# A graph-attention kernel on one core: 18 steps of layer 1 kept for the last change of layers, a spare PSUM bank, another order of the last closings, values by two node tiles

## The chip, the core and the metric

The kernel runs on one core of one Trainium2 chip. The core has five engines with instruction streams of their own: PE (TensorE, matmuls, with its weight loads shown apart as PEld), DVE (VectorE), ACT (ScalarE), POOL (GpSimd) and SP (SyncE, which here only issues DMAs). [...] The metric is the device time of one execution in microseconds (us); before the change it was 3778.08 us, the median of three runs (3776.47 to 3779.17).

## What is computed

Eight batches of 2048 nodes with 256 features go through two graph layers over one adjacency matrix. Cut to what matters:

```python
# layer 0: attention in 4 heads of 64, softmax inside each chunk of 256 keys, summed over 8 chunks
scores = clip(q @ k.T / 8, -10, 10); scores = where(adj == 0, -10, scores)
attn   = softmax(scores, over the 256 keys of a chunk)
y      = layernorm(sum over chunks of attn @ v, @ Wo + x)
x1     = layernorm(x + y)
# layer 1: graph attention, 4 heads of 64
Wh = x1 @ W;  e = leaky_relu(s_src[i] + s_dst[j], 0.2), -inf where adj == 0
h  = elu(softmax(e over j) @ Wh)
out = layernorm(x1 + h)
```

All is fp32. Each fp32 matmul of the program appears as two PE instructions in the profile.

## The kernel before

**Slots.** Layer 0 of a batch is cut into 64 slots (`SLOTS`): 4 query chunks `q` of 512 nodes, times 2 head pairs, times 8 key chunks. `i` is a slot's place in its query chunk, 0 to 15. Slot `s` issues the scores of slot `s + 1` (L385, tile `ps`), their clip and mask on DVE (L396, `pr`), `product(s, 0)` and `product(s, 1)` (L422, one for each head of the pair, tile `pc`), and between these the exponentials of slot `s + 1` on ACT (L408). ACT copies each `pc` out of PSUM (`raw`, L429); in the next slot DVE takes reciprocals of the sums (L437) and POOL multiplies and adds (L444, L446).

**Layer 1 rides along.** Layer 1 of batch `b - 1` (object `lower`, class `Layer1`) runs beside layer 0 of batch `b`. It has 8 units (2 halves of the nodes times 4 heads) of 16 tiles. A tile needs one DVE instruction (`make`, L741: `e` from `srow`, `gd` and the edge mask `et`) and 32 PE instructions (`use`, L763, tile `pa`). `step` makes two tiles and uses two; `make` stays two tiles ahead. At the end of a unit, ACT copies `pa` to `sums` (L775) and a generator `close` is put on `lower.tail`: its five pieces (`dn` L788 and L789, two lots of four scalings L795, exponential and relu L800 and L801, and `h` L803 on DVE) are taken one at a time by `rest(1)`, the first thing that each `step` does.

**Change of layers.** After slot 63 a written list `order` interleaves the last query chunk's output, norms and values, `factors` (three pieces: the last, `rows`, stores the rows of layer 1 to DRAM and has POOL scale `waug`, L686 and L688) and, for batches 0 to 6, the projections of the next batch. For the last batch (7) there is no next batch: slots 50 to 63 run without layer 1 steps (`LATE = 14`), and these 14 steps of batch 6's layer 1 stand in `order` instead; the last of them and `rest(5)`, which finishes the tail, come after `rows`. Then a new `Layer1` is built. Its constructor issues, on SP and in this order, three edge loads (L723) and one row load `srow` (L712). An edge buffer (4 of them) comes free when the two tiles that read it are made.

**Layer 1 alone.** The layer 1 of batch 7 then runs by itself, 64 steps, with the closings of batch 6 (`CLOSING_ALONE`) and of batch 7's first half (`ENDING`) between its steps. A closing of a group of 512 nodes loads `x1g`, adds it to `h` (L828), takes statistics (L487, L490, L495 to L498) and applies them (L502), then stores. Groups 2 and 3 of batch 7 need the last unit and are closed after step 63.

**Values.** The class `Between` holds what follows a query chunk's attention. Its `values(us)` multiplies `x1T` by layer 1's weights (L581, tile `pw`) and has ACT copy the result to `waug` (L588) and `sd` (L592). For one node tile, `pw` lies in bank `psM`; for two, in one of the two-bank tiles.

**PSUM.** `two_banks` turns between `psA0` and `psA1` (two banks each: `ps`, `pp`, `pv`, `po` of four tiles, `pw` of two tiles). `psC` is one bank for `pc`. `one_bank` turns between `psL0` and `psL1`, which hold `pa` whenever layer 1 runs. `psM` is one bank for `po` of two tiles, `pw` of one tile, and the small products of the change of layers. In batch 0, where no layer 1 runs, `product(s, 1)` takes `one_bank`; in all other slots both products take `psC` in turn.

Of the kernel before, what the change touches and what calls it, by code (L numbers as in the profile page):

```python
# [8 lines left out]
F32 = mybir.dt.float32  # L9
# [4 lines left out]
AF = mybir.ActivationFunctionType  # L14
ALU = mybir.AluOpType
AX = mybir.AxisListType

P = 128
CH = 512
# [3 lines left out]
def adj_resnorm_kernel(  # L23
# [19 lines left out]
    nc = tc.nc  # L43
    B, N, F = x.shape
    H, D = a_src.shape
    NT = N // P
# [3 lines left out]
    D1 = D + 1  # L50
# [5 lines left out]
    QT = CH // P  # L56
# [8 lines left out]
    SLOTS = NCH * QS  # L65
    UNITS = [(m, h) for m in range(len(BANKS)) for h in range(H)]
    FIRST = [sum(BANKS[:m]) for m in range(len(BANKS))]
    TILES = len(UNITS) * NT
    STEP = TILES // SLOTS
    LATE = 14  # L70
    WIDE = max(BANKS)
    JG = 2
    AHEAD_E = 3
# [31 lines left out]
    def two_banks(shape, name):  # L105

        turn_of[0] ^= 1
        return psA.tile(shape, F32, tag=f"psA{turn_of[0]}", name=name)

    def one_bank(shape, name, kind=F32):  # L110

        bank_of[0] ^= 1
        return psL.tile(shape, kind, tag=f"psL{bank_of[0]}", name=name)


    qT = big.tile([P, KC, N], F32, tag="qT", name="qT")
# [85 lines left out]
    def send():  # L202
        while outgoing:
            outgoing.pop(0)()
# [202 lines left out]
        pr = probs[s][u]  # L407
        nc.scalar.activation(pr, pr, AF.Exp, scale=0.125)  # L408

    def product(s, k, alone):  # L410
        q, hp, c = where[s]
        if k == 0:
            raws[s] = small.tile([P, 2, QT, D1], F32, tag="raw", name="raw")

        if alone and k:
            pc = one_bank([P, QT, D1], "pc")
        else:
            pc = psC.tile([P, QT, D1], F32, tag="psC", name="pc")
        for i in range(QT):
            for u in range(KT):  # L420
                for z in range(2):
                    nc.tensor.matmul(  # L422
                        pc[z * D : (z + 1) * D, i, :],
                        lhsT=probs[s][u][:, k, i * P + z * D : i * P + (z + 1) * D],
                        rhs=vaug[:, KT * c + u, 2 * hp + k, :],
                        start=(u == 0),
                        stop=(u == KT - 1),
                    )
        nc.scalar.copy(raws[s][:, k], pc)  # L429
# [81 lines left out]
    class Between:  # L511
# [60 lines left out]

        def values(self, us):
            n, t = len(us), QT * self.g + us[0]
            if n == 1:
                pw = psM.tile([P, 1, CH], F32, tag="psM", name="pw")
            else:
                pw = two_banks([P, 2, CH], "pw")
            for k, u in enumerate(us):
                for c in range(KC):  # L580
                    nc.tensor.matmul(  # L581
                        pw[:, k, : F + 2 * H],
                        lhsT=self.x1T[:, c, u * P : (u + 1) * P],
                        rhs=w1_sb[:, c, :],
                        start=(c == 0),
                        stop=(c == KC - 1),
                    )
            nc.scalar.copy(  # L588
                self.waug[:, t : t + n, :, :D],
                pw[:, :, :F].rearrange("p k (h d) -> p k h d", h=H),  # L590
            )
            nc.scalar.copy(  # L592
                self.sd[:, :, t : t + n], pw[:, :, F : F + 2 * H].rearrange("p k x -> p x k")
            )
# [16 lines left out]
        4: lambda o: o.output((2, 3)),  # L611
        7: lambda o: o.a.apply(o.y),
        11: lambda o: o.finish(),
        14: lambda o: o.values((0,)),
        15: lambda o: o.values((1,)),
    }

    WIDE_BESIDE = {
# [16 lines left out]
    }  # L635
    LATER_AHEAD = {0: lambda o: o.load()}
    LATER_BESIDE = {2: lambda o: o.turn()}
    LATER_BEHIND = {i: lambda o, i=i: o.values((i - 5,)) for i in range(5, 9)}

    BESIDE_0 = {i: steps for i, steps in BESIDE.items() if i != 14} | {15: BESIDE[14]}  # L640
    BEHIND_0 = {i: step for i, step in BEHIND.items() if i != 14} | {15: BEHIND[14]}

    def factors(b, sd, waug):

# [52 lines left out]
    class Layer1:  # L697
# [54 lines left out]
        def use(self):  # L752
            k = self.used
            n, j = k // NT, k % NT
            m, h = UNITS[n]
            if j == 0:
                self.pa = [
                    psL.tile([P, QT, D1], F32, tag=f"psL{i}", name="pa") for i in range(n_banks)
                ]
            e = self.e.pop(k)  # L760
            for i in range(BANKS[m]):
                for z in range(2):
                    nc.tensor.matmul(  # L763
                        self.pa[i // QT][z * D : (z + 1) * D, i % QT, :],
                        lhsT=e[:, i * P + z * D : i * P + (z + 1) * D],
                        rhs=self.waug[:, j, h, :],
                        start=(j == 0 and i % QT == 0),
                        stop=(j == NT - 1 and i % QT == QT - 1),
                        skip_group_check=True,
                    )  # L770
            self.used += 1
            if j == NT - 1:
                raw = small.tile([P, WIDE, D1], F32, tag="sums", name="sums", bufs=1)
                for i, pa in enumerate(self.pa):
                    nc.scalar.copy(raw[:, i * QT : (i + 1) * QT, :], pa)  # L775
                self.tail.append(self.close(n, raw))
# [41 lines left out]
    class Close:  # L818
# [12 lines left out]
        def finish(self):  # L831
            o = blocks.tile([P, QT, F], F32, tag="y", name="o")
            self.n.apply(o)
            outgoing.append(lambda: nc.sync.dma_start(out=by_node(out, self.b, self.g), in_=o))

    class Closing:


# [3 lines left out]
        def do(self, s, beside=True, behind=True):  # L842
            for g, step in self.table.get(s, ()):
                if step == "load" and behind:
                    self.of[g] = Close(self.b, g)
                elif step == "finish" and behind:
                    self.of[g].finish()
                elif step == "add" and beside:
                    self.of[g].add()
                elif step == "stats" and beside:  # L850
                    self.of[g].n.stats((0, 1, 2, 3))


    masks = Masks()
# [6 lines left out]
    for g in range(NCH):  # L861
        _, _, keys, values, queries = groups[g]
# [48 lines left out]
        39: [(1, "add")],  # L911
        40: [(0, "finish"), (1, "stats")],
        42: [(1, "finish")],
        SLOTS - 1: [(2, "load"), (3, "load")],
        SLOTS: [(2, "add"), (2, "stats"), (3, "add"), (3, "stats"), (2, "finish"), (3, "finish")],
    }
    lower = None
    for b in range(B):
# [15 lines left out]
        for s in range(SLOTS):  # L934
# [5 lines left out]
            if i == 0:  # L940
                before = group
                group = Between(b, q - 1, sd, waug) if q else None
                wide = 0 < q < NCH - 1
                ahead = {} if wide else AHEAD
                if wide:
                    beside, behind = WIDE_BESIDE, WIDE_BEHIND
                else:
                    beside, behind = (BESIDE, BEHIND) if b else (BESIDE_0, BEHIND_0)
                later_beside, after = (LATER_BESIDE, LATER_BEHIND) if q > 1 else ({}, {})
            if before and later_beside and i in LATER_AHEAD:  # L950
                LATER_AHEAD[i](before)
# [24 lines left out]
                    step(group)  # L976
            elif closing:
                closing.do(s, behind=False)
            product(s, 0, not lower)
            if s + 1 < SLOTS:  # L980
                for u in range(KT):
                    exps(s + 1, u)
# [2 lines left out]
                    lower.step()  # L985
            elif masks.left():
                masks.step()
            product(s, 1, not lower)

            if before and i in after:  # L990
                after[i](before)
# [35 lines left out]
        if b + 1 < B:  # L1027
            (k0, v0, q0), (l1, t1, k1, v1, q1), (l2, t2, k2, v2, q2), (l3, t3, k3, v3, q3) = turns
            rest = [lambda: lower.rest(1)] if lower else []
            first = [] if b else [lambda: before.values((1,))]  # L1030
            order = [begin, *rest, l1, *rest, *first, lambda: before.values((2, 3))]
            order += [*rest, ctx, *rest, *rest, k0]
            order += [steps[0], t1, steps[1], v0, steps[2], steps[3], l2, k1, steps[4], q0]
            order += [steps[5], v1, t2, l3, steps[6], q1, steps[7], k2, steps[8], steps[9], t3, v2]
            order += [lambda: [load_slab(s) for s in range(3)], fs[0], q2, fs[1], k3, fs[2], v3]
            order += [lambda: scores(0), q3, lambda: [exps(0, u) for u in range(KT)]]
        else:

            step = lower.step
            order = [begin, lambda: before.values((2, 3)), steps[0], step, ctx, step, steps[1], step]  # L1040
            order += [steps[2], step, steps[3], step, steps[4], step, steps[5], step, steps[6], step]
            order += [steps[7], step, steps[8], step, steps[9], step, fs[0], step, fs[1], step, fs[2]]
            order += [step, lambda: lower.rest(5)]
            assert sum(p is step for p in order) == LATE
        for piece in order:
            send()
            piece()
        send()
        lower = Layer1(b, gd, waug)

    closing, ending = Closing(B - 2, CLOSING_ALONE), Closing(B - 1, ENDING)
    closing.do(-1)
    for _ in range(STEP):
        lower.make()
    for s in range(SLOTS + 1):
        send()
        if s < SLOTS:
            lower.step()
        else:
            lower.rest(5)  # L1060
        closing.do(s)
        ending.do(s)
    send()


# [40 lines left out]
```

## Time and profile before

| what | value |
|---|---|
| median of three runs | 3778.08 us |
| the profiled execution | 3776.29 us |
| its span, first to last instruction | 3774.5 us |
| granted TensorE clock, mean | 0.993 |
| slots of batch 7, with what lies before them in that batch | 3134.1 to 3516 us |
| change of layers after batch 7 | 3516 to 3577.8 us |
| layer 1 of batch 7 alone | 3577.8 to 3755.6 us |
| last closings, to the end of the span | 3755.6 to 3774.5 us |

The profile is of one execution; times in it count from the span's start. A row of the timeline gives start, length, engine, line, operation, the tile written and the tiles read, how many instructions were merged, and in brackets the engine's idle time just before, with what ended it. Matmuls overlap one another, so the mean length of one says nothing of their rate; the distance between the starts of two groups does. In the chain of waits, overlaps are cut out, so its lengths add up.

### The profile page before, as it was taken

To read this page: it belongs to the slowest core of one execution; us is meant where nothing else is said; L and a number is where in the kernel's file an instruction comes from. 1 tells how busy PE (TensorE), PEld (TensorE's weight loads), DVE (VectorE), ACT (ScalarE), POOL (GpSimd) and SP (SyncE) were. 2 spreads that over 40 slices of the span, in tenths; PEclk is the share of its full clock that TensorE was granted. 3 is DMA by queue.
4 is the path that set the end of the run, shared out by engine and by line. 5 is a ranking of instruction groups with operands and counts; after the bars stand their busy time and mean duration, and the time that the engine had idled before them with its cause. 6 is when DMAs were issued, how large, how long until landed. Compare 5 with 4: busy or idle time off the path is not lost.

```text
span 3774.5 us, 159666 instructions
## 1 busy us (share of the span) xinstructions
PE 3664.0 (97%) x72100; PEld 2741.3 (73%) x72100; DVE 3133.7 (83%) x4202; ACT 1988.0 (53%) x3665; POOL 1365.5 (36%) x1202
## 2 busy tenths in 40 slices
PE   9999999999999999999999999999999999999786
PEld 5656677776777777776777767777677777776676
DVE  5877489986999689895998959988699977988798
ACT  4666455555555555555555545555455555555322
POOL 1445234333433343333443324433334333334300
PEclk9999999999999999999999999999999999999998
DMA  6652333333333343333433334333433333433354
GB/s 163 152 117 69 78 98 109 105 75 112 106 108 105 86 119 102 104 93 88 133 97 98 100 89 135 109 100 78 113 107 107 105 80 112 115 97 84 95 154 128
DMA packets 672060, 398.46 MB, mean 106 GB/s; under 512 B 427280, under 2 KB 591504, under 8 KB 671376
## 3 DMA queue, kind: packets, MB, share of 16 engines
q1 hardware_dynamic: 621376, 354.54, 35.6%
q10 hardware_dynamic: 50000, 33.70, 2.8%
q8 instruction: 564, 9.24, 1.0%
q14 instruction: 120, 0.98, 0.1%
HBM read 331.22 MB, written 56.89 MB: 103 GB/s over the span
## 4 chain that ended last, share of the span: by engine, by line
PE 86%; DVE 5%; issue 3%; ACT 3%; DMA 1%; POOL 1%; SPq 0%; ACTq 0%; DVEq 0%; POOLq 0%
PE pc L422 26%; PE ps L385 24%; PE pa L763 22%; PE pp L329 5%; PE po L537 3%; PE pw L581 3%; PE pv L345 2%; DVE e L741 2%; ACT y L502 1%; DVE pr L396 1%; ACT pr L408 1%; DMA xp<-in_x_dram 0%; PE pm L246 0%; ACT qT L337 0%; SPq L279 0%
## 5 line engine op out<-in xcount | busy, mean ns | idle before, releaser
L396 DVE SCALAR_TENSOR_TENSOR pr<-ps,slab 128x1024 f32<-128x1024 f32 x1024 | 1194.3, 1207 | 211.1 <-PE ps L385 207.7
L422 PEld LDWEIGHTS pc<-vaug,pr 128*64 128x64 f32 x32768 | 1039.5, 138 | 406.4 <-issue 313.6
L741 DVE SCALAR_TENSOR_TENSOR e<-srow,gd,et 128x1024 f32<-128x1024 f32 x1024 | 1273.1, 1286 | 10.4 <-PE pa L763 5.8
L422 PE MATMUL pc<-vaug,pr 128*64 128x65 f32 x32768 | 1155.9, 224 | 14.3 <-ACT raw L429 7.7
L763 PE MATMUL pa<-waug,e 128*64 128x65 f32 x32768 | 1069.8, 224 | 41.0 <-DVE e L741 36.4
L763 PEld LDWEIGHTS pa<-waug,e 128*64 128x64 f32 x32768 | 1015.1, 139 | 60.1 <-DVE e L741 45.5
L408 ACT ACTIVATE pr<-pr 128x1024 f32<-128x1024 f32 x1024 | 1038.2, 1055 | 32.8 <-DVE pr L396 26.4
L385 PE MATMUL ps<-qT,kT 64*128 64x512 f32 x4096 | 1023.2, 616 | 3.5 <-DVE pr L396 2.9
L429 ACT COPY raw<-pc 128x260 f32<-128x260 f32 x1024 | 380.5, 372 | 1222.7 <-PE pc L422 1178.7
L444 POOL TENSOR_TENSOR part<-raw,rd 128x512 f32<-128x512 f32 x448 | 467.9, 1044 | 1407.5 <-DVE rd L437 1389.4
L446 POOL TENSOR_TENSOR acc<-acc,part 128x512 f32<-128x512 f32 x448 | 575.0, 1283 | 35.2
L385 PEld LDWEIGHTS ps<-qT,kT 64*128 64x128 f32 x4096 | 349.9, 186 | 326.6 <-issue 229.6
L437 DVE RECIPROCAL rd<-raw 128x8 f32<-128x8 f32 x512 | 100.8, 197 | 132.1 <-ACT raw L429 129.6
L444 POOL TENSOR_TENSOR acc<-raw,rd 128x512 f32<-128x512 f32 x64 | 66.7, 1043 | 339.3 <-DVE rd L437 339.3
L581 PE MATMUL pw<-w_sb,x1T 128*128 128x264 f32 x512 | 139.8, 409 | 6.1 <-DVE x1T L291 5.0
L795 ACT ACTIVATE sums<-sums,dn 128x64 f32<-128x64 f32 x512 | 134.0, 337 | 9.7 <-DVE dn L789 9.3
L497 POOL TENSOR_TENSOR rs_c<-rs_c,nhalf 128x4 f32<-128x4 f32 x32 | 54.0, 1687 | 223.8 <-DVE off_c L496 223.8
L537 PE MATMUL po<-wo_sb,qT 128*128 128x256 f32 x512 | 125.5, 390 | 3.1 <-DVE qT L464 2.8
L329 PE MATMUL pp<-xT,wk_sb 128*128 128x512 f32 x256 | 119.3, 609 | 7.9 <-ACT qT L337 6.6
L329 PE MATMUL pp<-xT,wq_sb 128*128 128x512 f32 x256 | 116.2, 597 | 0.0
L345 PE MATMUL pv<-wv_sb,xT 128*128 128x256 f32 x512 | 115.9, 379 | 0.0
L581 PEld LDWEIGHTS pw<-w_sb,x1T 128*128 128x128 f32 x512 | 92.4, 193 | 27.5 <-DVE x1T L291 5.3
(94 smaller groups left out, 1853.1 us busy)
## 6 DMA issues: line engine op xcount, KB each, us to landing
et<-edgeD SPq DMA_DIRECT2D x512, 256.0 KB, 3.1
slab<-clipD SPq DMA_DIRECT2D x512, 128.0 KB, 3.1
srow<-rowD SPq DMA_DIRECT2D x64, 512.0 KB, 5.0
xg<-in_x_dram SPq DMA_DIRECT2D x32, 512.0 KB, 5.3
x1D<-y ACTq DMA_DIRECT2D x32, 512.0 KB, 4.4
x1g<-x1D SPq DMA_DIRECT2D x32, 512.0 KB, 5.2
out_dram<-o SPq DMA_DIRECT2D x32, 512.0 KB, 3.3
ctxD<-acc ACTq DMA_DIRECT2D x56, 256.0 KB, 2.5
```

The costliest lines, as they stand in the source:

```text
L329: nc.tensor.matmul(pps[c], lhsT=w[:, kc, c * P : (c + 1) * P], rhs=st["xT"][:, kc, :], start=(kc == 0), stop=(kc == KC - 1),)
L385: nc.tensor.matmul(ps[:, k, :], lhsT=kT[rows, hp, t * P : (t + 1) * P], rhs=qT[rows, hp, cols], start=True, stop=True,)
L396: nc.vector.scalar_tensor_tensor(pr, pss[u], -CLIP, slab[:, u, :].unsqueeze(1).to_broadcast([P, 2, CH]), op0=ALU.max, op1=ALU.min,)
L408: nc.scalar.activation(pr, pr, AF.Exp, scale=0.125)
L422: nc.tensor.matmul(pc[z * D : (z + 1) * D, i, :], lhsT=probs[s][u][:, k, i * P + z * D : i * P + (z + 1) * D], rhs=vaug[:, KT * c + u, 2 * ...
L429: nc.scalar.copy(raws[s][:, k], pc)
L444: nc.gpsimd.tensor_mul(part, raw[:, :, :, :D], rd.to_broadcast([P, 2, QT, D]))
L446: nc.gpsimd.tensor_add(accv, accv, part)
L537: nc.tensor.matmul(po[:, k, :], lhsT=qT[:, c, t * P : (t + 1) * P], rhs=wo_sb[:, c, :], start=(c == 0), stop=(c == KC - 1),)
L581: nc.tensor.matmul(pw[:, k, : F + 2 * H], lhsT=self.x1T[:, c, u * P : (u + 1) * P], rhs=w1_sb[:, c, :], start=(c == 0), stop=(c == KC - 1),)
L741: nc.vector.scalar_tensor_tensor(e[:, :w], self.rows[n][:, :w], self.gd[:, h, j : j + 1], self.edge[k // JG][:, j % JG, :w], op0=ALU.max, ...
L763: nc.tensor.matmul(self.pa[i // QT][z * D : (z + 1) * D, i % QT, :], lhsT=e[:, i * P + z * D : i * P + (z + 1) * D], rhs=self.waug[:, j, h ...
```

## The change

Five edits:

1. `LATE` goes from 14 to 18: slots 46 to 63 of batch 7 have no layer 1 step, and 18 steps stand in the last `order`. Five of them, in place of one and `rest(5)`, come after the last piece of `factors`. The tail that is left of the old layer is handed to the new `Layer1`.
2. In those 18 slots `product(s, 1)` writes to `psM` (`spare_bank`) and not to `psC`. Batch 0 keeps `one_bank`.
3. `values` always takes `two_banks`. It is called for two node tiles at once: `(0, 1)` in slot 15 of the last query chunk (before: `(0,)` in slot 14, `(1,)` in slot 15), and `(0, 1)` in slot 5, `(2, 3)` in slot 7 for a chunk that is finished later (before: one tile in each of slots 5 to 8). In batch 0 the second of the two early values no longer stands in `order`.
4. The last unit of the last batch gets no copy to `sums` and no `close`. A new generator `last` works on each of its two `pa` banks straight from PSUM, the two interleaved, and only for the last head's 64 features; it takes the statistics, and applies them by turns on ACT and DVE, storing two node tiles at a time.
5. `ENDING`: the loads of groups 2 and 3 move from step 63 to step 59, and their addition of `x1g` for the first three heads (`add_most`) goes to steps 62 and 63.

```diff
-    LATE = 14
+    LATE = 18
...
+    def spare_bank(shape, name):
+        return psM.tile(shape, F32, tag="psM", name=name)
...
-            if n == 1:
-                pw = psM.tile([P, 1, CH], F32, tag="psM", name="pw")
-            else:
-                pw = two_banks([P, 2, CH], "pw")
+            pw = two_banks([P, n, CH], "pw")
...
-        14: lambda o: o.values((0,)),
-        15: lambda o: o.values((1,)),
+        15: lambda o: o.values((0, 1)),
...
-    LATER_BEHIND = {i: lambda o, i=i: o.values((i - 5,)) for i in range(5, 9)}
+    LATER_BEHIND = {5: lambda o: o.values((0, 1)), 7: lambda o: o.values((2, 3))}
...
-            if j == NT - 1:
+            if j == NT - 1 and not (self.b == B - 1 and n == len(UNITS) - 1):
...
+        def add_most(self):
+            f = slice(0, (H - 1) * D)
+            nc.vector.tensor_add(self.h[:, :, f], self.h[:, :, f], self.x[:, :, f])
+
+        def last(self, pa):
+            f = slice((H - 1) * D, F)
+            dn = small.tile([P, QT, 1], F32, tag="dn", name="dn")
+            nc.vector.tensor_scalar(dn, pa[:, :, D:D1], 1e-30, None, ALU.max)
+            nc.vector.reciprocal(dn, dn)
+            hh = small.tile([P, QT, D], F32, tag="raw", name="hh")
+            nc.vector.tensor_mul(hh, pa[:, :, :D], dn.to_broadcast([P, QT, D]))
+            ee = small.tile([P, QT, D], F32, tag="ee", name="ee")
+            nc.scalar.activation(ee, hh, AF.Exp)
+            hp = small.tile([P, QT, D], F32, tag="acc", name="hp")
+            nc.vector.scalar_tensor_tensor(
+                hp, hh, 0.0, self.x[:, :, f], op0=ALU.max, op1=ALU.add
+            )
+            yield 1
+            nc.vector.scalar_tensor_tensor(
+                self.h[:, :, f], ee, 1.0, hp, op0=ALU.min, op1=ALU.add
+            )
+            self.n = Norm(self.h, "c")
+            self.n.stats(tuple(range(QT)))
+            yield 1
...
+            for k in range(QT):
+                rs, off = self.n.rs[:, k : k + 1], self.n.off[:, k : k + 1]
+                src, dst = self.h[:, k, :], o[:, k, :]
+                if k % 2:
+                    nc.vector.tensor_scalar(dst, src, rs, off, ALU.mult, ALU.add)
+                    nc.sync.dma_start(out=to[:, k - 1 : k + 1, :], in_=o[:, k - 1 : k + 1, :])
+                else:
+                    nc.scalar.activation(dst, src, AF.Identity, bias=off, scale=rs)
...
-        SLOTS - 1: [(2, "load"), (3, "load")],
-        SLOTS: [(2, "add"), (2, "stats"), (3, "add"), (3, "stats"), (2, "finish"), (3, "finish")],
+        59: [(2, "load"), (3, "load")],
+        62: [(2, "most")],
+        63: [(3, "most")],
...
-            product(s, 1, not lower)
+            if not lower:
+                product(s, 1, one_bank)
+            elif b + 1 < B or s < SLOTS - LATE:
+                product(s, 1)
+            else:
+                product(s, 1, spare_bank)
...
-            first = [] if b else [lambda: before.values((1,))]
-            order = [begin, *rest, l1, *rest, *first, lambda: before.values((2, 3))]
+            order = [begin, *rest, l1, *rest, lambda: before.values((2, 3))]
...
-            order += [step, lambda: lower.rest(5)]
+            order += [step] * 5
...
+        undone = lower.tail if lower else []
         lower = Layer1(b, gd, waug)
+        lower.tail += undone
...
+    ends = [ending.of[2 + k].last(pa) for k, pa in enumerate(lower.pa)]
+    for _ in range(3):
+        for end in ends:
+            next(end, None)
```

More of the change, by code (lines that the diff above doesn't have):

```diff
@@ L408, in exps, with product @@
         nc.scalar.activation(pr, pr, AF.Exp, scale=0.125)
-    def product(s, k, alone):
+    def product(s, k, spare=None):
         q, hp, c = where[s]
@@ L413, in product @@
             raws[s] = small.tile([P, 2, QT, D1], F32, tag="raw", name="raw")
-        if alone and k:
-            pc = one_bank([P, QT, D1], "pc")
+        if spare:
+            pc = spare([P, QT, D1], "pc")
         else:
@@ L637, in adj_resnorm_kernel @@
     LATER_BESIDE = {2: lambda o: o.turn()}
-    LATER_BEHIND = {i: lambda o, i=i: o.values((i - 5,)) for i in range(5, 9)}
+    LATER_BEHIND = {5: lambda o: o.values((0, 1)), 7: lambda o: o.values((2, 3))}
     BESIDE_0 = {i: steps for i, steps in BESIDE.items() if i != 14} | {15: BESIDE[14]}
-    BEHIND_0 = {i: step for i, step in BEHIND.items() if i != 14} | {15: BEHIND[14]}
     def factors(b, sd, waug):
@@ L834, in finish @@
             outgoing.append(lambda: nc.sync.dma_start(out=by_node(out, self.b, self.g), in_=o))
+        def add_most(self):
[21 more added lines that the diff above has]
+            yield 1
+            o = blocks.tile([P, QT, F], F32, tag="y", name="o")
+            to = by_node(out, self.b, self.g)
+            for k in range(QT):
[6 more added lines that the diff above has]
+                    nc.scalar.activation(dst, src, AF.Identity, bias=off, scale=rs)
     class Closing:
@@ L851, in do @@
                     self.of[g].n.stats((0, 1, 2, 3))
+                elif step == "most":
+                    self.of[g].add_most()
     masks = Masks()
@@ L947, in adj_resnorm_kernel @@
                 else:
-                    beside, behind = (BESIDE, BEHIND) if b else (BESIDE_0, BEHIND_0)
+                    beside, behind = BESIDE if b else BESIDE_0, BEHIND
                 later_beside, after = (LATER_BESIDE, LATER_BEHIND) if q > 1 else ({}, {})
@@ L978, in adj_resnorm_kernel @@
                 closing.do(s, behind=False)
-            product(s, 0, not lower)
+            product(s, 0)
             if s + 1 < SLOTS:
@@ L1054, in adj_resnorm_kernel @@
         lower.make()
-    for s in range(SLOTS + 1):
+    for s in range(SLOTS):
         send()
[L1057 to L1060, printed above, removed]
+        lower.step()
         closing.do(s)
```

## The prediction, made before the changed kernel ran

> **What bounds the kernel now.** I read the page's busy table first, then the chain of waits, then the windows by stage, and last the timeline of the stages that the change touches.
>
> ```profile
> PE 3664.0 (97%) x72100; PEld 2741.3 (73%) x72100; DVE 3133.7 (83%) x4202; ACT 1988.0 (53%) x3665; POOL 1365.5 (36%) x1202
> PE 86%; DVE 5%; issue 3%; ACT 3%; DMA 1%; POOL 1%; SPq 0%; ACTq 0%; DVEq 0%; POOLq 0%
> ```
>
> PE is the path over most of the span, so a microsecond saved on PE there is one off the total. The windows (us, then busy time and instructions of PE, PEld, DVE, ACT, POOL, then granted clock, DMA share, GB/s) show where it is not:
>
> ```profile
> 3442.70:3507.40 64.70, 58.02 (x900) 38.17 (x898) 42.26 (x66) 36.05 (x67) 29.86 (x27) 1.00 0.21 52
> 3507.40:3566.00 58.60, 50.11 (x1011) 43.83 (x1011) 46.78 (x66) 19.01 (x47) 12.42 (x10) 0.91 0.29 86
> 3566.00:3577.80 11.80, 3.38 (x95) 2.84 (x91) 6.63 (x8) 4.82 (x16) 9.46 (x5) 0.85 0.57 183
> 3577.80:3754.40 176.60, 150.91 (x4064) 134.90 (x4064) 175.57 (x214) 40.37 (x108) 13.48 (x12) 0.95 0.49 149
> 3754.40:3774.50 20.10, 1.17 (x34) 1.01 (x32) 7.27 (x26) 8.17 (x20) 3.32 (x4) 0.60 0.15 53
> ```
>
> The last slots of batch 7 leave PE 6.7 us idle, the end of the change of layers 8.4 us; layer 1 alone is DVE's (175.57 of 176.60 us); the end is one chain of small steps.
>
> **1. Values by two tiles (edit 3).** From the chain of waits:
>
> ```profile
> 1671.30 1.09 PE pw L581 x4
> 3553.66 1.98 PE pw L581 x8
> ```
>
> Four instructions cost the path 1.09 us, eight 1.98, not 2.18[...]. A pair saves 0.20 us. There are 5 pairs in a batch (two in chunks 2 and 3 each, one in slot 63). Batches 0 to 6 save 35 x 0.20 = 7.0 us; batch 7's first two 0.4, its others are counted in part 2. **-7.4.**
>
> What could eat it: `pw` now takes a two-bank tile, so the second `ps` of the next scores waits for ACT's copies of `pw`, and behind that `ps` the whole PE stream waits. Existing copies of two tiles end 0.70 us after the matmuls (3555.64 to 3556.34). The second `ps` starts 0.96 us into its scores, about 0.9 after those matmuls end. ACT is idle then: in the slot that starts at 3436.88 its last exponential ends at 3442.33, a tail's scalings at 3443.28, `raw` at 3443.54, and `pw` would end near 3444.7. So I cost it at nothing; the cover is 0.13 us plus ACT's idle microsecond.
>
> **2. Slots 46 to 63 of batch 7 (edits 1, 2).** A slot with layer 1 takes 5.80 us. Without it, it took 4.68 (3488.40 to 3493.08 in the chain), with this wait on the single `psC`:
>
> ```profile
> 3446.28 1.15 PE L422 MATMUL pc<-vaug,pr 128*64 128x65 f32 x32 [0.53 <-ACT raw L429]
> ```
>
> Batch 0 has the second bank already, and its slots after the masks show what is left: PE without a gap, a slot in 3.93 us (354.36 to 358.29):
>
> ```profile
> 354.36 1.99 PE L385 MATMUL ps<-qT,kT 64*128 64x512 f32 x8
> 356.28 2.09 PE L422 MATMUL pc<-vaug,pr 128*64 128x65 f32 x64
> 358.29 1.99 PE L385 MATMUL ps<-qT,kT 64*128 64x512 f32 x8
> ```
>
> But `psM` also carries `po`. Counting from a score's start T: the exponentials end at T+5.45, and ACT's copy of the second product stands behind them, so it ends near T+5.8. In slot 51 `po` must wait for it and the slot ends at 8.0 us in place of 6.61. In slot 52 the product waits for DVE's addition of `po`, behind two masks (T+4.26), and the second `po` again for the copy: 7.8 in place of 6.61. Slot 53: 4.26 + 1.01 + 1.98 = 7.25. The others: nine of 3.93; 4.54, 4.00 and 4.54 where ACT's application of a norm (2.08 us) delays the exponentials, as in batch 0 (300.62 to 305.16); 3.93 + 1.98 = 5.91 for slot 55, and 0.6 for its norm. Sum 78.0, against 87.9 before (3419.48 to 3507.38). After that nothing is left between the last scores and the last products to cover the exponentials: +0.1. **-9.8.** Ends: -14 if the waits on `psM` vanish, -4.5 if the slots stay at 4.68.
>
> **3. The change of layers (edit 1).** Four steps more after `rows`. On DVE alone eight `e` at 1.195 us (3577.605 to 3578.801) cost 9.6 us, and the 8.04 us gap of PE would cover them:
>
> ```profile
> 3567.43 8.51 POOL L688 TENSOR_TENSOR waug<-waug,ed 128x1024 f32<-128x1024 f32 x4
> 3574.09 2.39 DVE L803 SCALAR_TENSOR_TENSOR h<-ee,sums 128x512 f32<-128x512 f32 x1 [3.47 <-ACT sums L801]
> 3577.83 7.29 PE L763 MATMUL pa<-waug,e 128*64 128x65 f32 x192 [8.07 <-DVE e L741]
> ```
>
> Yet POOL scales `waug` just then. `h`, usually 0.68 us, took 2.39: it started with POOL's fourth multiplication and ended after it. At 3517 the same in a row:
>
> ```profile
> 3516.97 1.85 POOL L444 TENSOR_TENSOR part<-raw,rd 128x512 f32<-128x512 f32 x1 [1.03 <-DVE rd L437]
> 3517.83 2.07 DVE L741 SCALAR_TENSOR_TENSOR e<-srow,gd,et 128x1024 f32<-128x1024 f32 x1
> 3518.89 2.14 POOL L446 TENSOR_TENSOR acc<-acc,part 128x512 f32<-128x512 f32 x1
> ```
>
> 1.85 for 1.04, 2.07 for 1.28, 2.14 for 1.28: the two engines alternate. [...] Before, only two `e` met these multiplications. By the rows without it the steps add 9.6 us of DVE; with it each of four multiplications adds the 1.71 to 1.75 us that `h` shows, 7.0 in all. I take it.
>
> So from 3568.5 (last `e` before): six `e` 7.2, POOL 7.0, the old tail's `h` 0.6: 3583.3. Only then does SP get the third edge buffer, and in its queue the new `srow` stands behind that load: issue at 3583.85. This first row landed 4.03 us after its issue (3569.18). First new `e` at 3587.95, before at 3576.41: **+11.5.** An extra unit boundary adds about what leaves with the old tail's `h`. Ends: +4.4 without the alternation, +14 if the row takes the 6.5 us that is the longest shown.
>
> **4. Layer 1 alone.** The old tail's `dn` (0.17 + 0.20) and `h` (0.68) now stand in DVE's full queue: **+1.05**. The moved loads have three steps to land. `add_most` comes after the last `e`.
>
> **5. The end (edits 4, 5).** Before: 20.1 us from the last `e` (3754.40). Now, from it: two `add_most` of 768 elements at 0.93 (1.22 for 1024, 0.68 for 512), 1.85, while PE finishes at 1.2; two first phases of four small DVE instructions, 2 x 1.05; two of `h` 0.33 and statistics 1.94; together 8.5. Then POOL's power 1.01 and product 0.26, two ACT applications 1.0, and a store with about 3.4 from issue to the end of the span (3.9 shown for twice the bytes): 14.5 with the waits between. **-5.6**, ends -3 and -7.
>
> **Sum:** -7.4 - 9.8 + 11.5 + 1.05 - 5.6 = -10.2 us. The profiled execution (3776.29 us, span 3774.5) becomes 3766; the median lies 1.8 us above it, so 3768 for the median.
>
> **Rivals.**
> - **No alternation, the gap really filled.** POOL's multiplications slip between the `e` at little cost: part 3 is +4.4, the total -17: **3761**. For it: in this trace the `e` that met POOL's first scaling took 1.307 us. Against: that `e` had started first, and POOL took 2.88 then.
> - **A slow PE clock eats the moved steps.** With a tile only every 2.9 us PE is idle for most of it, as it was before this window:
>
> ```profile
> 3577.00:3582.00 5.00, 4.17 (x92) 4.20 (x94) 4.85 (x5) 0.00 (x0) 0.00 (x0) 0.60 0.16 52
> ```
>
> There a tile took 1.79 us (3.57 for two) in place of 1.2: 0.6 on each of some ten tiles: total -4, **3774**. Against: while DVE alternates, 1.79 still fits into 2.9.
> - **Slower: the paired values stall the next scores.** Place: the second `ps` after each of 32 pairs (the 8 in slot 63 have none behind). If an exponential (1.05 us) stands before the copies, a pair loses up to 0.9 us; at 0.6 it is +19, total +9: **3787**. It decides from 0.55 us a pair. Against: ACT's idle time above; for: every batch repeats it.
> - **The bank does not do what it says:** slots stay near 4.68; total -5, 3773.
>
> **Chances.** The sum as forecast 0.55 (its own range 3764 to 3772), no alternation 0.17, slow clock or idle bank 0.20, stalled values 0.08. A measurement of this kernel tells 0.2%, 7.6 us, from no change. Of the forecast's 0.55 I put 0.09 within that, of the second group all: faster 0.63, same 0.29, slower 0.08. The range leaves the stalled values out and reaches to both other cases: 3760 to 3776.
>
> **What would show it.** Slots of 7.78 and 5.80 us where four of 6.89 stood in batches 1 to 6; 3.93 between scores in batch 7 after slot 46, with waits of `po` on `raw` and of `pc` on `y` in slots 51 to 53; `e` of 2.9 us pitch beside four long L688; `srow` issued after the last-but-two `e` and the first new `e` 11 to 12 us later than before; 14 to 15 us after the last `e`. I am wrong if the `e` keep their 1.2 us pitch beside POOL, if slots with paired values exceed 7.8, or if the end takes 18.

## The result, and the profile after

The changed kernel takes 3768.2 us (median of 19 runs), the kernel before 3776.5 us in the runs beside it: a ratio of 0.9979, with a 95% interval of 0.9972 to 0.9985. That is 8 us off the total, at the predicted 3768. The profiled execution has a span of 3764.9 us, 9.6 less than before.

The page's rows for the engines and for the chain of waits look almost as before:

```profile
PE 3655.7 (97%) x72100; PEld 2743.7 (73%) x72100; DVE 3138.5 (83%) x4213; ACT 1979.9 (53%) x3571; POOL 1368.3 (36%) x1202
PE 84%; DVE 7%; issue 4%; ACT 3%; DMA 1%; SPq 0%; ACTq 0%; POOL 0%; DVEq 0%; POOLq 0%
```

The chain's DVE share went from 5 to 7%, some 77 us. Followed stage by stage, 39 of these lie in the slots of batch 7, where DVE had none before, 18 ahead of batch 7 and only 11 in the change of layers. The totals say little, because gains and losses cancel in them; the windows by stage show them apart (us, then busy time and instructions of PE, PEld, DVE, ACT, POOL, then granted clock, DMA share, GB/s). The last slots of batch 7, then the change of layers cut in two, and the end:

```profile
3426.20:3489.50 63.30, 57.69 (x900) 38.00 (x898) 41.89 (x66) 36.99 (x61) 28.75 (x27) 0.97 0.21 51
3489.50:3550.80 61.30, 50.52 (x1066) 44.24 (x1064) 49.72 (x71) 21.68 (x54) 15.93 (x13) 0.94 0.31 90
3550.80:3571.10 20.30, 12.44 (x290) 11.79 (x288) 17.14 (x11) 1.75 (x4) 9.88 (x4) 0.75 0.37 101
3749.80:3764.90 15.10, 1.19 (x34) 1.01 (x32) 9.84 (x37) 3.01 (x6) 2.62 (x4) 0.67 0.20 71
```

Before the first new `e` there was a stretch of 11.8 us with PE busy for 3.4 and DVE for 6.6 of them. Now it is 20.3 us, with PE busy for 12.4, at a granted clock of 0.75, and DVE for 17.1. The end went from 20.1 to 15.1. Put beside the terms of the prediction, each stage measured in the two profiles from one event to the next:

| term | stage | before | after | measured | predicted |
|---|---|---|---|---|---|
| 1 | start to the first scores of batch 7 | 3134.1 | 3124.6 | -9.5 | -7.0 |
| 1 | from there to the scores of slot 47 | 285.4 | 285.0 | -0.4 | -0.4 |
| 2 | scores of slot 47 to those of slot 63 | 87.9 | 79.9 | -8.1 | -9.8 |
| 3 | scores of slot 63 to the first new `e` | 69.0 | 81.6 | +12.6 | +11.5 |
| 4 | first new `e` to the end of the last | 178.0 | 178.8 | +0.8 | +1.05 |
| 5 | last `e` to the end of the span | 20.1 | 15.1 | -5.0 | -5.6 |
| | sum | | | -9.6 | -10.2 |

### The profile page after: what moved, and what is told of

It is laid out like the page before. It is cut to its first block, busy times and chain, and to the rows that moved or that the text cites. A ratio compares the mean times of both kernels' runs of the same rounds, so it can differ in the third digit from the quotient of the medians.

```text
span 3764.9 us, 159631 instructions
## 1 busy us (share of the span) xinstructions
PE 3655.7 (97%) x72100; PEld 2743.7 (73%) x72100; DVE 3138.5 (83%) x4213; ACT 1979.9 (53%) x3571; POOL 1368.3 (36%) x1202
## 4 chain that ended last, share of the span: by engine, by line
PE 84%; DVE 7%; issue 4%; ACT 3%; DMA 1%; SPq 0%; ACTq 0%; POOL 0%; DVEq 0%; POOLq 0%
PE pc L425 25%; PE ps L388 23%; PE pa L761 21%; PE pp L332 5%; PE pw L581 3%; PE po L540 3%; DVE e L739 3%; PE pv L348 2%; DVE pr L399 2%; ACT y L505 1%; ACT pr L411 1%; DVE y L560 0%; DMA xp<-in_x_dram 0%; DVE y L557 0%; ACT qT L340 0%
## 5 line engine op out<-in xcount | busy, mean ns | idle before, releaser
L425 PE MATMUL pc<-vaug,pr 128*64 128x65 f32 x32768 | 1153.6, 224 | 15.1 <-ACT pr L411 9.6
L581 PE MATMUL pw<-w_sb,x1T 128*128 128x264 f32 x512 | 128.0, 398 | 4.7 <-DVE x1T L294 4.7
```

The costliest lines, as they stand in the source:

```text
L425: nc.tensor.matmul(pc[z * D : (z + 1) * D, i, :], lhsT=probs[s][u][:, k, i * P + z * D : i * P + (z + 1) * D], rhs=vaug[:, KT * c + u, 2 * ...
L581: nc.tensor.matmul(pw[:, k, : F + 2 * H], lhsT=self.x1T[:, c, u * P : (u + 1) * P], rhs=w1_sb[:, c, :], start=(c == 0), stop=(c == KC - 1),)
```

## The experiments

Ten further kernels ran, each beside the kernel before, whose median lay between 3776.2 and 3776.7. The interval of one ratio is between ±0.0006 and ±0.0017, some 2 to 6 us, so a difference of a few microseconds between two experiments is read from the stages of their profiles, with the medians beside them. The medians:

| kernel | median, us | ratio to before, 95% interval |
|---|---|---|
| edit 3 alone | 3767.7 | 0.9977 (0.9967 to 0.9986) |
| edits 4 and 5 alone | 3772.1 | 0.9989 (0.9983 to 0.9996) |
| edits 3, 4, 5 | 3762.4 | 0.9962 (0.9948 to 0.9975) |
| edits 2 to 5 (`LATE` stays 14) | 3758.4 | 0.9952 (0.9940 to 0.9965) |
| all: the changed kernel | 3768.2 | 0.9979 (0.9972 to 0.9985) |
| changed, row before the edges | 3765.3 | 0.9968 (0.9956 to 0.9980) |
| changed, without POOL's last scaling | 3762.2 | 0.9961 (0.9947 to 0.9975) |
| `LATE = 16`, other bank, row first | 3756.7 | 0.9946 (0.9932 to 0.9961) |
| `LATE = 10` | 3756.9 | 0.9948 (0.9933 to 0.9963) |
| `LATE = 8`, other bank | 3760.7 | 0.9957 (0.9940 to 0.9973) |
| `LATE = 14`, `psC` in slots 51 to 53 | 3756.6 | 0.9947 (0.9932 to 0.9962) |

### Edit 3 alone

The kernel before with the values in pairs and nothing else:

```diff
-            if n == 1:
-                pw = psM.tile([P, 1, CH], F32, tag="psM", name="pw")
-            else:
-                pw = two_banks([P, 2, CH], "pw")
+            pw = two_banks([P, n, CH], "pw")
...
```

> The kernel before with edit 3 alone: values by two node tiles. My theory ([...]0.20 us, 5 pairs in each of 8 batches, and in batch 0 two waits of 0.27 us on the single bank go): 8 to 9 us faster than before, ratio 0.9976 to 0.9979; slots of 7.78 and 5.80 us where four of 6.89 stood. Rival (the last third of the chain, not the pairs, brought the gain): within 2 us of before.

It gave 8.6 us in the medians: as much as the whole change. So the other four edits together come to nothing that the medians show, and the rest of the study is about why. The chain of waits of the changed kernel shows the scores of three slots, in the batch of the prediction's rows (start, us, engine, tile):

```profile
1667.46 1.92 PE ps L388 x8
...
1673.26 1.92 PE ps L388 x8
...
1681.04 1.92 PE ps L388 x8
```

From 1667.46 to 1673.26 is 5.80 us, a slot without values; from there to 1681.04, 7.78, a slot with a pair: 27.16 us for two of each, where four of 6.89 make 27.56. Nothing stalls the next scores. With 0.31 for the pair of slot 63, an undisturbed batch gains 1.10 us, where the prediction had 1.0. What in a group of four costs the 0.20 us was not shown.

### Edits 4 and 5 alone

From the changed kernel, edit 3 is undone as well as

```diff
-    LATE = 18
+    LATE = 14
...
-            elif b + 1 < B or s < SLOTS - LATE:
-                product(s, 1)
-            else:
-                product(s, 1, spare_bank)
+            else:
+                product(s, 1)
...
-            order += [step] * 5
+            order += [step, lambda: lower.rest(5)]
```

> The kernel before with edits 4 and 5 alone (the end). My theory: the end costs 15.1 us after the last e in every kernel with these edits and 20.1 in every kernel without, whatever stands ahead of it, and two additions of 768 elements beside the last steps cost at most 0.8: total -4.2 to -5.0 us, a ratio of 0.9987 to 0.9989, all stages before the last e as before. Rival: the additions delay the last e and give the gain back: total within 1.5 us of before.

Median -4.1 us, profile -4.3: the end takes 15.5 us and every stage before it is as before to 0.3 us. The theory holds at its lower edge, where the median misses 4.2 by 0.1, well inside its interval; the additions beside the last steps delay nothing visible (178.03 us of layer 1 alone, before 177.99).

### The four moved steps put back

```diff
-    LATE = 18
+    LATE = 14
...
-            order += [step] * 5
+            order += [step]
```

> The changed kernel with 14 steps kept back in place of 18, all else as changed. My theory (the four moved steps cost more in the change of layers than they free in the slots): the slots 46 to 49 take 6.6 us more, the first new e comes 12 to 14 us earlier after the last product of slot 63, net 5 to 7 us faster than the changed kernel, so 13 to 15 us faster than before (ratio about 0.9963). Rival (the steps fill a gap that was idle anyway): about 6 us slower than the changed kernel, 2 us faster than before.

The net was larger than expected: -9.8 us in the medians, -8.5 in the profiles. There it is -14.0 in the change of layers (67.6 in place of 81.6) against +4.7 in the slots, where 6.6 was expected, and +0.6 in layer 1 alone. So the moved steps lost 8 to 10 us, and the idle of PE that they were to fill was no free place. The timeline of this kernel shows what lies in it (start, length, engine, line, operation, tiles, shapes, count, idle before and its releaser):

```profile
3554.19 8.51 POOL L686 TENSOR_TENSOR waug<-waug,ed 128x1024 f32<-128x1024 f32 x4
3557.66 0.32 SPq L710 DMA_DIRECT2D srow<-rowD  x1
3561.96 3.02 DVE L739 SCALAR_TENSOR_TENSOR e<-srow,gd,et 128x1024 f32<-128x1024 f32 x2 [6.65 <-DMA srow<-rowD]
```

PE idles because DVE waits 6.65 us for the new row, and the row is in flight while POOL scales. With 18 kept steps DVE has four more steps of `e` to make before the third edge buffer, and with it the row, can be asked for, and makes them against POOL (four `e` took 8.21 us, shown below).

### The spare bank undone too

The kernel of the section above, with edit 2 taken back as well:

```diff
-            elif b + 1 < B or s < SLOTS - LATE:
-                product(s, 1)
-            else:
-                product(s, 1, spare_bank)
+            else:
+                product(s, 1)
```

> The kernel with LATE = 14 and one step after rows, and edit 2 undone as well: both products of the last slots take psC as before. So edits 3, 4 and 5 alone. My theory: slots 46 to 61 take 87.5 us as in the kernel with the pairs alone (84.6 with the spare bank and LATE = 14), the change of layers stays at 67.5, so the spare bank is worth 3.0 us at LATE = 14: 3761 to 3762 in the median. Rival: what the bank gains in the slots is lost again before the change of layers: 3758 to 3759, the same as with the bank.

3762.4 in the median, just above the expected band: the bank is worth 3.0 us in the slots (87.5 against 84.55) and 4.1 in the medians. Not all of the rest is noise: the change of layers was 1.1 us shorter here, as the new row landed earlier, but the first two new `e` then met POOL's last multiplications (2.05 and 2.94 us), and layer 1 alone took 1.9 more. The rival is out by the profiles, in which the bank's gain in the slots isn't lost again; the medians' intervals overlap. This makes a ladder of the medians: pairs -8.6, end about -5, bank about -4, and then the four moved steps +9.8.

### POOL's scaling left out

```diff
-            for h in range(H):
+            for h in range(H if b + 1 < B else 0):
```

> The changed kernel without POOL's four multiplications of waug in batch 7 (layer 1 of the last batch then uses unscaled values). My theory (e and these multiplications take turns): the e after the last piece of factors keep a pitch of 1.2 us, the first new e comes 7 us earlier, total 6 to 7 us faster than the changed kernel. Rival (the e are late because PE at a low clock holds their buffers): at most 2 us faster.

The scaling belongs to the computation, so of this kernel only the time counts. The total fell by 6.0 us in the medians and by 4.7 in the profiles. The timeline of the changed kernel, DVE and POOL at the change of layers:

```profile
3548.36 8.21 DVE L739 SCALAR_TENSOR_TENSOR e<-srow,gd,et 128x1024 f32<-128x1024 f32 x4
3549.75 10.93 POOL L686 TENSOR_TENSOR waug<-waug,ed 128x1024 f32<-128x1024 f32 x4
3556.50 2.40 DVE L801 SCALAR_TENSOR_TENSOR h<-ee,sums 128x512 f32<-128x512 f32 x1
3558.82 6.53 DVE L739 SCALAR_TENSOR_TENSOR e<-srow,gd,et 128x1024 f32<-128x1024 f32 x4
```

and DVE's `e` in the kernel without the scaling:

```profile
3549.63 4.90 DVE L739 SCALAR_TENSOR_TENSOR e<-srow,gd,et 128x1024 f32<-128x1024 f32 x4
3555.05 7.25 DVE L739 SCALAR_TENSOR_TENSOR e<-srow,gd,et 128x1024 f32<-128x1024 f32 x6
3565.78 2.48 DVE L739 SCALAR_TENSOR_TENSOR e<-srow,gd,et 128x1024 f32<-128x1024 f32 x2 [3.48 <-DMA srow<-rowD]
```

Four `e` take 4.90 us alone and 8.21 beside POOL. From the start of these four to the first new `e` it is 22.7 us with the scaling and 16.15 without, and both times the row comes last (2.49 us of wait, shown below, and 3.48). So the alternation's price is 6.6 us, put at 7.0. Counted from the scores of slot 63, the last old `e` ends only 5.7 us earlier (73.4 in place of 79.1) and the first new one starts 4.7 earlier, because this execution came to the first of the four `e` 1.85 us later than the changed kernel's; the next section shows where that arises.

### The row ahead of the edges

```diff
+            self.load_row(0)
...
-            self.load_row(0)
```

The call moves ahead of the three edge loads in the constructor.

> The changed kernel with the new layer's row load issued ahead of its three edge loads. My theory (the row stood in SP's queue behind an edge buffer that the last-but-two e releases): the row is issued some 14 us earlier, the first new e starts right behind the last old one, 2.5 us earlier than in the changed kernel, total 2 to 3 us faster than the changed kernel. Rival (the wait is for something else that lands at the same time): no change.

From the start of ACT's copy of the new rows (`flat`, L682), which goes before their store, to the first new `e` it was 21.3 us in the changed kernel and is 18.8 here; the 2.5 us that the row's place in SP's queue costs come out as expected, and -2.9 in the medians, whose intervals overlap. Counted from that copy the row is issued 13 us earlier. In the profiled execution the stage as a whole gained only 0.3, because an earlier place of it lost some 2 us: the first transposes of `acc` waited 1.57 us for POOL,

```profile
3506.80 0.66 PE L473 MATMUL pt<-identf,acc 128*128 128x128 f32 x4 [1.57 <-POOL acc L449]
```

and in the changed kernel's execution they did not wait. The kernel without the scaling has the same 1.57 us. In both, DVE's transpose into `x1T` (L294), ahead of this place, waited for a load, 1.16 us here and 1.49 there; in the changed kernel it did not. What DVE had behind it then fell among other instructions of POOL. So the turns of DVE and POOL differ from one execution to the next; in these three the difference goes with the landing of a load.

### In search of a better version

Three kernels vary how many steps are kept. The first has 16, the other banks for the second product, and the row first:

```diff
-    LATE = 18
+    LATE = 16
...
+            self.load_row(0)
...
-            self.load_row(0)
...
-                product(s, 1, spare_bank)
+                product(s, 1, one_bank)
...
-            order += [step] * 5
+            order += [step] * 3
```

> The changed kernel with 16 steps kept back (a unit of layer 1 then ends just before slot 48, so the two banks of pa are free), the second product of slots 48 to 63 in these two banks in place of psM, and the row load ahead of the edge loads. My theory (psM costs slots 51 to 53 about 4 us, and each moved step that meets POOL's multiplications costs more than it frees): slots 51 to 53 take 18.9 us together as in batch 0, not 22.9 to 24.8; the change of layers 5 us longer than with 14 steps; total 3756 to 3758. Rival (the bank is not what holds slots 51 to 53): they take 22 us or more, total 3760 or more.

Near what was expected on all counts: slots 51 to 53 took 18.59 us, the change of layers 73.4, 5.8 more than with 14 steps. With `psL`, free in these slots, nothing of `po` waits for the second product: its waits in slots 51 to 53 are 0.38 us for `qT` and 0.27 for `y`. What each of the three differences gives to the total was not tried.

With 10 kept steps, no step follows `steps[5]`, `steps[8]` or the first two pieces of `factors`, and one stands after the last piece:

```diff
-    LATE = 18
+    LATE = 10
...
-            order += [steps[2], step, steps[3], step, steps[4], step, steps[5], step, steps[6], step]
-            order += [steps[7], step, steps[8], step, steps[9], step, fs[0], step, fs[1], step, fs[2]]
-            order += [step] * 5
+            order += [steps[2], step, steps[3], step, steps[4], step, steps[5], steps[6], step]
+            order += [steps[7], step, steps[8], steps[9], step, fs[0], fs[1], fs[2]]
+            order += [step]
```

> The changed kernel with 10 steps kept back; the four that go back to the slots are those after the norm's application, after its second statistics, after the first pair of values and the one before the last piece of factors. psM then serves slots 54 to 63, where nothing else uses it. My theory (DVE, not a lack of PE work, sets the change of layers, and layer 1 steps in slots 51 to 53 are free beside the waits on psM): slots 50 to 53 take 2 to 4 us more than with 14 steps, the change of layers 7 to 9 us less, total 3752 to 3755. Rival (the steps cover PE's waits in the change of layers): no faster than with 14 steps, 3758 or more.

A miss in size: 3756.9. Against 14 steps the change of layers fell by 4.2 us only, while the slots rose by 2.25. The chain of waits of this kernel shows the floor:

```profile
3552.47 2.97 DMA rowD<-flat
3555.45 4.29 DMA srow<-rowD
3559.82 1.29 DVE e L739
```

The rows are stored to DRAM (2.97 us) and fetched again (4.29); DVE has nothing left to do and, by the timeline, waits 8.02 us for `srow`. Fewer steps cannot shorten that. With 8 (and `one_bank`):

```diff
-    LATE = 18
+    LATE = 8
...
-                product(s, 1, spare_bank)
+                product(s, 1, one_bank)
...
-            order += [steps[2], step, steps[3], step, steps[4], step, steps[5], step, steps[6], step]
-            order += [steps[7], step, steps[8], step, steps[9], step, fs[0], step, fs[1], step, fs[2]]
-            order += [step] * 5
+            order += [steps[2], step, steps[3], step, steps[4], steps[5], steps[6], step]
+            order += [steps[7], steps[8], steps[9], step, fs[0], fs[1], fs[2]]
+            order += [step]
```

> The changed kernel with 8 steps kept back and the second product of slots 56 to 63 in the two banks of pa, free there because a unit ends before slot 56. My theory: two more steps leave DVE's queue in the change of layers (4 us) and cost the slots 3.7 us: within 2 us of the kernel with 10 steps. Rival (the steps cover PE's waits): slower than with 10 steps by 3 us or more.

The change of layers stays (63.2 against 63.4 with 10) and the slots cost 3.7 more: 3760.7. The rival, that the steps between the pieces cover waits of the chain, was right here: ACT's copy of the rows starts 55.7 us after the scores of slot 63 with 8 steps and 55.8 with 10, so the two steps had not held it up. From 14 steps to 10 it had come 3.7 us earlier.

### `psC` again where `po` needs its bank

```diff
-    LATE = 18
+    LATE = 14
...
-            elif b + 1 < B or s < SLOTS - LATE:
+            elif b + 1 < B or s < SLOTS - LATE or i in (3, 4, 5):
...
-            order += [step] * 5
+            order += [step]
```

> The changed kernel with 14 steps kept back, as in e2_late14, and both products in psC again in slots 51, 52 and 53, where psM carries po. My theory (psM is the bank that po waits for and that the product waits for): the three slots take 19.9 us in place of 22.9, total 3 us less than e2_late14, 3755. Rival (a product in psC costs the same 0.5 us of waiting there, and nothing is gained): 3758.

Slots 51 to 53 took 19.87 us, with 14 steps and `psM` 22.85: 3.0 less for these slots in the profile, and 1.8 less in the medians of the total. The wait of the product on `psC` is back and is the smaller evil: 0.53 us before a `pc`, where `psM` has 1.76 before a `po` (2.08 with 18 steps, shown below).

The versions at 3756.6 to 3756.9 beat the changed kernel by 11 to 12 us and the one before by 20; which of the three is fastest, these runs do not tell.

## Why the prediction was right, by its own steps

**Values by two tiles: right, too small by up to 2.5 us in a profile.** Batches 1 to 6 gave 1.1 us each on average (0.74 to 1.46), near the 1.0 of the sum. Batch 0 was counted like the others. It gained 2.7 in the changed kernel's profile and 2.2 with edit 3 alone, most of it in its change of layers, where PE's clock was low (0.50, shown below) and edit 3 took a piece out of `order`. PE's timeline there, before:

```profile
379.66 2.13 PE L581 MATMUL pw<-w_sb,x1T 128*128 128x264 f32 x4 [5.00 <-DVE x1T L291]
382.33 4.82 PE L581 MATMUL pw<-w_sb,x1T 128*128 128x264 f32 x12 [0.54 <-ACT sd L592]
386.98 0.60 PE L470 MATMUL pt<-identf,acc 128*128 128x128 f32 x4
```

and after:

```profile
378.71 5.51 PE L581 MATMUL pw<-w_sb,x1T 128*128 128x264 f32 x16 [4.75 <-DVE x1T L294]
384.06 0.60 PE L473 MATMUL pt<-identf,acc 128*128 128x128 f32 x4
```

From the values to the transposes 7.32 us became 5.35: the 0.54 wait for the one bank is gone, and a group. But most of this difference is not the edit's. The clock was at half of full for 6.8 us before and for 3.4 us after, and in the kernel with `psC` again in slots 51 to 53, which has the pairs too, for 6.8 again (windows, in this order of the three kernels):

```profile
379.37:386.18 6.81, 5.98 (x13) 4.21 (x14) 1.54 (x3) 0.89 (x4) 2.31 (x2) 0.50 0.82 154
379.05:382.45 3.40, 3.40 (x9) 2.68 (x8) 0.77 (x1) 0.09 (x1) 2.15 (x2) 0.50 1.01 230
377.99:384.80 6.81, 6.23 (x14) 4.89 (x15) 1.83 (x3) 0.66 (x2) 2.30 (x2) 0.50 0.87 154
```

There the way from the values to the transposes took 6.72 us, and batch 0 gained 0.9 in all; the kernel without the scaling gained 1.1. By estimate from these, the edit is worth about 1 us in batch 0 as well, and the rest goes with the shorter stretch of half clock (3.4 us in place of 6.8), which the sum had not looked for. What remains of the spread (seven batches gave 7.2 with edit 3 alone and 9.5 here) are single delays of 0.2 to 0.8 us in various batches of one profile and not of another.

**The slots: right in kind, -8.1 in place of -9.8.** All the waits named came: `po` on `raw`, `pc` on `y`. PE's timeline, from the end of slot 51 on:

```profile
3436.19 2.66 PE L540 MATMUL po<-wo_sb,qT 128*128 128x256 f32 x8 [2.08 <-ACT raw L432]
3438.78 2.96 PE L388 MATMUL ps<-qT,kT 64*128 64x512 f32 x8
...
3444.00 1.15 PE L425 MATMUL pc<-vaug,pr 128*64 128x65 f32 x32 [1.18 <-DVE y L551]
```

Slots 51 to 53 took 8.67, 8.77 and 7.34 us where 8.0, 7.8 and 7.25 were worked out. The kernel without POOL's scaling, the same up to there, took 8.01, 7.82 and 7.34: the waits were sized rightly, and the excess of 1.6 us goes with PE's clock, which the sum took as full: it was 0.50 for 3.41 us of slots 51 and 52, and 1.00 in the kernel without the scaling (both in the last section). The kernel with the row first took 9.35, 8.11 and 7.34. Most other slots came at 3.93, and slot 55 at 5.91, as predicted.

**The change of layers: right, +12.6 in place of +11.5.** The alternation happened (the 2.40 us of `h`, the four long multiplications; 6.6 us, put at 7.0), the row was stuck behind the edge load, and SP issued it 76.3 us after the scores of slot 63, where the working gives 76.5 (3583.85 less 3507.38; PE's gap of 8.04 us in that working is 8.07 in its own line):

```profile
3565.75 0.42 SPq L710 DMA_DIRECT2D srow<-rowD  x1
...
3571.08 2.48 DVE L739 SCALAR_TENSOR_TENSOR e<-srow,gd,et 128x1024 f32<-128x1024 f32 x2 [2.49 <-DMA srow<-rowD]
```

The mis-sized term is the row: from issue to the first `e` 5.3 us, where 4.1 was taken from one earlier row. That was the fastest of the sixteen from batch 7 on in the profile before, whose median is 5.1 us from issue to landing. That the whole came within 1.1 us is in part luck: the kernels with the row first and without the scaling came to ACT's copy of the rows some 2 us later than this execution did.

**Layer 1 alone: right**, +0.8 for +1.05.

**The end: right**, -5.0 for -5.6. The small instructions that were scaled from larger shapes were too cheap: `h` of 256 elements was put at 0.33, and the timeline has 0.42 for it, as for `hh`, `hp` and ACT's exponential. What edit 4 and edit 5 do apart was not tried.

**The rivals.** No alternation: refuted, by the 8.21 us above against 4.90. An idle bank: refuted by the slots at 3.93. Stalled values: refuted, no slot with a pair exceeds 7.78 in batches 1 to 6. A slow clock did cost, but in slots 51 and 52 (0.50 for 3.41 us, with the 1.6 us above). In the moved steps DVE waited for PE twice (0.25 and 0.41 us, at a granted clock of 0.75), and these waits ended before the row landed, so they cost nothing.

The prediction had the signs and nearly the sizes, and its sum comes out as losses and gains that offset each other: the errors of the five terms, -2.5, +1.7, +1.1, -0.3 and +0.6, add up to +0.6. That it is so little is partly luck: the first two, the largest, go mostly with stretches of half clock, 3.4 us in place of 6.8 in batch 0 and 3.41 us on top in slots 51 and 52.

## What to carry to other kernels

An idle stretch on the busiest engine is not a place to put work into before it is known what the other engines do in it: here it held POOL's scaling and a row's way through DRAM, and work that needs DVE and an edge buffer delayed both and lost 8 to 10 us. Where two producers share one PSUM bank, count what each must wait for in its slot: three slots of 16 gave back 3.0 of the 5.9 us that the bank gained in the others. When several edits come together, run them apart: the pairing of matmul groups was worth the whole, and leaving out the moved steps more than doubled the gain.

## What the runs showed of the hardware beyond the expected

The same pause of PE, 2.08 us before `po` in slot 51, was followed by a low clock in the changed kernel and not in the one without the scaling, whose program is the same up to there. In the changed kernel (columns as in the windows by stage; the pause lies in the first row, from 3434.1 to 3436.19):

```profile
3433.97:3437.38 3.41, 1.33 (x12) 1.06 (x7) 1.63 (x3) 2.09 (x3) 1.90 (x2) 1.00 0.14 38
3437.38:3440.79 3.41, 3.41 (x10) 1.65 (x10) 0.00 (x0) 0.00 (x0) 1.51 (x2) 0.50 0.02 5
```

PE was busy for 1.33 us of the first row at a granted clock of 1.00 and for all of the second at 0.50, where a group of scores took 2.96 us. In the kernel without the scaling (the pause ends at 3437.23):

```profile
3430.00:3435.00 5.00, 5.00 (x114) 3.66 (x110) 4.70 (x6) 3.41 (x6) 3.33 (x4) 1.00 0.47 112
3435.00:3437.00 2.00, 0.15 (x6) 0.01 (x2) 1.44 (x2) 1.93 (x3) 1.11 (x1) 1.00 0.03 8
3437.00:3441.00 4.00, 3.77 (x16) 2.13 (x16) 0.88 (x2) 0.18 (x1) 2.30 (x2) 1.00 0.11 33
3441.00:3445.00 4.00, 2.38 (x66) 2.06 (x64) 2.28 (x3) 2.65 (x4) 0.00 (x0) 1.00 0.11 33
```

The clock was 1.00 throughout, and the same group of scores took 1.99 us. Slots 51 and 52 together took 17.4 us with the low clock and 15.8 without, 1.6 less. What decides between the two was not shown.

Open is also why the load ahead of the first transposes, and with it the order of turns between DVE and POOL, comes 1.2 to 1.5 us earlier or later in executions of one program.
